# Four batches of a group through both attention layers in one sequence, the projections' row carried through DRAM

## Chip, cores and metric

The kernel runs on one core of a Trainium2 chip (trn2). The metric is device time in microseconds (us), the median of several runs; lower is better. Everything is computed in fp32. PE is the matrix engine, DVE the vector engine, ACT the scalar engine, POOL the engine that issues gathers and scatters here, SP the engine whose queue issues most plain DMAs.

## What is computed

The input is x (16 batches, 1024 nodes, 256 features) and one 1024 x 1024 adjacency matrix with about 17 entries a row. Four layers follow each other:

```python
# layer 0: a score for every edge, then sums over edges
S   = sigmoid(relu(x@W1[:d] (+) x@W1[d:] + b1) @ W2 + b2)      # per pair of nodes
x   = beta1*x + beta2*((S*adj)^T @ x @ Wa + ba) + beta3*(((adj^T @ x) * x) @ Wm + bm)
# layer 1
x   = x + relu((adj @ x) @ W^T + b)
# layers 2 and 3: attention over all pairs, adj as an additive bias
f   = x @ W1^T                       # features
f1  = f @ W2 + b2                    # one number a node: its projection
c   = softmax(leaky_relu(f1[i] + f1[j]) + adj)
x   = c @ f + bias2 + x
```

## The kernel before, in words

The 16 batches are handled in four groups of four (GB = 4). Three kinds of work share the core.

**The side work** (score_steps) computes the edge scores of layer 0. One step handles one edge slot of 128 nodes for the four batches of a group: POOL gathers 512 KB of neighbours' rows (L695), DVE adds and multiplies (L812, L814), ACT sums four times (L818), POOL scatters the scores into a dense matrix in DRAM (L700). There are 608 such steps, and 8 more that look for the slots. A step's gather is issued four steps ahead.

**The free part** (score_free) is dense matrix work of layer 0 that needs no scores, for all batches, on PE.

**The group part** runs for g = 0..3 once the scores of group g are in DRAM. with_edges multiplies the dense scores (DMA gd, turned into gc by ACT at L1072) with hw of four batches; its sums take all eight PSUM banks. Then pair_layers runs for batches 0 and 1 and again for 2 and 3: layer_one (projected, then neighbours, which reads adjT_in by DMA) and layers 2 and 3. For one batch and layer these consist of front (8 node tiles of features, 16 products of 257 columns; column 256 is the projection), scales and two calls of sums (v = 0, 1; 8 x 4 products each, on tiles m that DVE makes at L1044 from rho, tau and exp(adj)).

scales (L1003 to L1026) needs the projections of all nodes as a row on every partition (rho). It gets this by nine PE transposes of broadcast columns (eight at L1010 of feats, one at L1015 of their maxima), ACT evacuates two banks into rho (L1019), and exponentials and eight scalings of feats follow. finish at the end of sums divides by the softmax's sum: in layer 2 (second) the values are turned back by PE a little later (L1227), in layer 3 (third) z gets its bias, eight transposes of z (L1251) are issued after the last product, and the result goes out by a DMA on ACT's queue.

**Order.** The main work and the side work are Python generators. Side.along lets the main generator emit work, adds its own estimate of that work's us times a rate to what is owed, and emits so many side steps in between: 0.26 a us in the free part, 0.255 in all of the group part. Work that should not be emitted at once goes on a list, later, and catch_up emits all of it: at tile 1 of a front, or after tile 0 of a sums. A scheduler then puts the instructions into the engines' queues, roughly in that order but earlier where a tile is free and operands are there; each queue is served in order. paced ties a side step's DVE add, gc's copy and the loads of gd to a product on PE a few products back. For the next group, ahead loads hw and z of all four batches in the middle of the second pair; z's tiles are those of the current group (four tiles in all), so each load waits for its predecessor's last reader. gd has four tiles and is loaded by with_edges itself (only the first group's first four are loaded early). hw, y and feats share five tiles, rho has two, m four, adjT_in three.

The last group runs without side work, with another way for part of layer 1 (far_ahead, by_lists); its attention layers are the same pair_layers.

Of the kernel before, what the change touches and what calls it, by code (L numbers as in the profile page):

```python
# [13 lines left out]
ALU = mybir.AluOpType  # L14
# [5 lines left out]
RATE = (0.26, 0.255)  # L20
# [45 lines left out]
def gnn_stack_kernel(  # L66
# [120 lines left out]
    class Attention:  # L187


        def __init__(self, W1, W2, b2, bias2, name):  # L190
            self.W1 = W1
            self.w2 = column(W2, f"{name}_w2")
            self.b2 = everywhere(b2, 1, f"{name}_b2")
            self.bias2 = column(bias2, f"{name}_bias2c")
            self.wT = const.tile([P, DH, D + 1], F32, name=f"{name}_wT")
            self.rows = const.tile([P, DH, P], F32, name=f"{name}_rows")

        def prepare(self, nat):
# [8 lines left out]
            nc.vector.tensor_copy(self.wT[:, :, D], ps[:, :DH])  # L207
            for dh in range(DH):
                nc.vector.tensor_copy(self.rows[:, dh, :], self.wT[:, dh, D : D + 1].to_broadcast([P, P]))
# [26 lines left out]
    def prepare(t):  # L236
        transpose_weight(l1wT, t[:, 0])
        for i, gat in enumerate((gat2, gat3)):
            gat.prepare(t[:, 1 + i])
# [22 lines left out]
    part_d = dram.tile([XT * P + P, 2 * D], F32, name="part_d")  # L262

# [411 lines left out]
    with tc.If(listed > 0) as arm:  # L675
        with ExitStack() as stack:
# [192 lines left out]
            class Side:  # L869
# [5 lines left out]
                def along(self, main, rate=1):  # L875
                    for us in main:
                        self.owed += us * rate
# [35 lines left out]
            z_loads = []  # L913

            with ExitStack() as first:
# [48 lines left out]
                side.along(with_zeros(score_free()), RATE[0])  # L964
# [12 lines left out]
            def front(x, weights):  # L977

                wT = weights.wT
                f = ttile("feats").rearrange("p (t d) -> p t d", t=NT)  # L980
                for jt in range(NT):
# [7 lines left out]
                    if jt == 1:  # L989
                        catch_up()  # L990
                    yield 0.86
                made = {}
                later.append(lambda: scales(f, weights, made))
                return made

            def scales(f, weights, made):
# [4 lines left out]
                ta = small.tile([P, NT], F32, tag="tau", name="tau")  # L1001
# [16 lines left out]
                for v in range(NV):  # L1018
                    nc.scalar.activation(r[:, v * HN : (v + 1) * HN], banks[v], AF.Relu, bias=sh[:, 3:4])  # L1019
                nc.vector.tensor_scalar(sh[:, 1:2], sh[:, 0:1], -0.01, None, ALU.mult)  # L1020
# [8 lines left out]
            later = []  # L1029

            def catch_up():
                while later:
                    later.pop(0)()

            def sums(made, v, finish):

                if "f" not in made:
                    catch_up()
# [3 lines left out]
                for jt in range(NT):  # L1042
# [9 lines left out]
                    if jt == 0:  # L1052
                        catch_up()
# [10 lines left out]
            def with_edges(g, hw, z):  # L1064

                for v in range(N // QN):
# [33 lines left out]
            def projected(z, keep=None):  # L1100

                y = [node_major("y") for _ in range(2)]
# [24 lines left out]
            def neighbours(y, z, cols):  # L1127
                n = cols.stop - cols.start
                acc = [[bank() for _ in range(DH)] for _ in range(2)]
                for jt in range(NT):  # L1130
                    a = three.tile([P, HN], F32, tag="a", name="adjT_in")[:, :n]
                    nc.sync.dma_start(a, adjT_d[jt][:, cols])
                    for i in range(2):
                        for eh in range(DH):
# [3 lines left out]
                            )  # L1138
                    yield 3.4 * n / HN
# [66 lines left out]
            def pair_layers(b, z, ahead, first):  # L1206


                yield from first


                def second(i):
                    def finish(v, acc, share):
                        cols = slice(v * HN, (v + 1) * HN)
                        vals = []
                        for c in range(HT):
                            if c % 2 == 0:
                                pair = four.tile([P, 2, D], F32, tag="st", name="val")
                            val = pair[:, c % 2, :]
                            nc.scalar.activation(val, acc[c][:, :D], AF.Identity, scale=share[:, c : c + 1])  # L1220
                            vals.append(val)

                        def turn_back():
                            ps = [bank() for _ in range(DH)]
                            for c in range(HT):
                                for dh in range(DH):
                                    nc.tensor.transpose(  # L1227
                                        ps[dh][:, c * P : (c + 1) * P], vals[c][:, dh * P : (dh + 1) * P], ident
                                    )
                            for dh in range(DH):  # L1230
                                nc.vector.scalar_tensor_tensor(
                                    z[i][:, dh, cols], ps[dh], gat2.bias2[:, dh : dh + 1], z[i][:, dh, cols],
                                    ALU.add, ALU.add,
                                )
                        later.append(turn_back)
                    return finish


                def third(i):
                    def finish(v, acc, share):  # L1240
                        if v == 0:
                            for dh in range(DH):
                                nc.scalar.activation(
                                    z[i][:, dh, :], z[i][:, dh, :], AF.Identity, bias=gat3.bias2[:, dh : dh + 1]
                                )
                        for c in range(0, HT, 2):
                            ps = bank()
                            it = v * HT + c
                            for k in range(2):
                                for dh in range(DH):  # L1250
# [203 lines left out]
```

## Time and profile before

| what | us |
|---|---|
| median of 3 runs | 3181.08 (3177.64 to 3188.89) |
| the profiled execution | 3181.81 |
| its span, first to last instruction | 3180.1 |
| PE busy in it | 3117.1 |
| DVE busy | 2354.2 |
| ACT busy | 1946.7 |
| POOL busy | 1823.1 |
| granted PE clock | 0.994 of full |

The stages of the trace, from the span's start, in us: until 165 the start and the first group's inputs; 165 to 955 the free part with side work; then for each of groups 0, 1, 2 the edges (955 to 1139, 1526 to 1639, 2090 to 2203) and the two pairs (to 1526, 2090 and 2653); group 3's edges from 2653 to 2766, the rest of it to the end. Of a pair, about 68 us are layer 1 and about 150 the attention layers.

In lines of the profile, "out<-in" are the program's names, "x" the count, then busy us, mean ns of one, and the idle time of the engine just before these instructions with what ended it. A product in fp32 is recorded as two matmul rows; a transpose as one. Rows overlap: a row's duration is longer than the distance to the next row's start.

### The profile page before, as it was taken

How to read it: one execution, taken by the hardware profiler on the slowest of the kernel's cores; microseconds unless marked ns; L12 is line 12 of the kernel's file. 1: busy time of each engine (PE TensorE's matmuls, PEld its weight loads, DVE VectorE, ACT ScalarE, POOL GpSimd, SP SyncE). 2: the span in 40 equal slices, each digit the busy share in tenths (PEclk: the TensorE clock that was granted, in tenths of full speed). 3: DMA queues.
4: the chain of work that ended last, by engine and by line, in shares of the span. 5: the costliest groups of instructions: out<-in, count | busy, mean ns of one | idle time of the engine just before them, and what ended most of it. 6: DMA issues, size and time to landing. Idle time of an engine off the chain costs nothing.

```text
span 3180.1 us, 39242 instructions
## 1 busy us (share of the span) xinstructions
PE 3117.1 (98%) x12122; PEld 2198.4 (69%) x12122; DVE 2354.2 (74%) x3174; ACT 1946.7 (61%) x6512; POOL 1823.1 (57%) x1483
## 2 busy tenths in 40 slices
PE   8899999999999999999999999999999999999999
PEld 5444554545547768678876866888587688858888
DVE  7797777768775689889777978977798892147844
ACT  3245565656667877567886757788666774513342
POOL 1146778777665666767566665656676652067600
PEclk9999999999999999999999999999999999999999
DMA  9899798788889764766876576587657644476600
GB/s 314 292 324 327 253 304 278 257 256 251 259 284 332 226 185 136 225 189 198 294 240 177 155 205 188 181 294 238 193 142 216 187 133 159 133 253 170 165 7 28
DMA packets 281994, 687.48 MB, mean 216 GB/s; under 512 B 45280, under 2 KB 137440, under 8 KB 274608
## 3 DMA queue, kind: packets, MB, share of 16 engines
q0 software_dynamic: 128224, 387.80, 41.9%
q1 hardware_dynamic: 126112, 245.98, 22.4%
q10 hardware_dynamic: 27440, 51.13, 4.3%
q8 instruction: 97, 1.59, 0.2%
q14 instruction: 121, 0.99, 0.1%
HBM read 553.45 MB, written 131.32 MB: 215 GB/s over the span
## 4 chain that ended last, share of the span: by engine, by line
PE 78%; DVE 8%; DMA 6%; ACT 4%; issue 2%; POOL 1%; SPq 0%; ACTq 0%; DVEq 0%; POOLq 0%
PE bank L126 75%; DMA z<-v_d,slot_v 2%; DVE z L812 2%; ACT z L818 2%; DVE z L814 2%; ACT gc L1072 1%; DVE slot_a L440 1%; DMA gd<-dense_d 1%; PE bank L1227 1%; DVE left L442 1%; DVE m L1044 1%; PE bank L1010 1%; POOL z L695 1%; PE bank L1251 1%; POOL dense_d L700 1%
## 5 line engine op out<-in xcount | busy, mean ns | idle before, releaser
L818 ACT ACTIVATE z<-z 128x256 f32<-128x256 f32 x2432 | 979.9, 407 | 630.0 <-DVE z L814 611.1
L812 DVE TENSOR_TENSOR z<-z,u 128x1024 f32<-128x1024 f32 x608 | 738.6, 1220 | 416.6 <-PE bank L126 305.6
L126 PE MATMUL bank<-feats,m 128*128 128x257 f32 x4096 | 917.1, 381 | 5.2 <-DVE m L1044 4.5
L695 POOL DMA_INDIRECT z<-v_d,slot_v x512 | 644.3, 1258 | 447.0 <-ACT z L818 255.7
L126 PEld LDWEIGHTS bank<-feats,m 128*128 128x128 f32 x4096 | 767.7, 190 | 122.1 <-DVE m L1044 8.0
L700 POOL DMA_INDIRECT dense_d<-gt,slot_at x512 | 645.8, 1261 | 187.2 <-issue 135.8
L814 DVE SCALAR_TENSOR_TENSOR z<-z,w2r 128x1024 f32<-128x1024 f32 x608 | 737.7, 1219 | 9.0
L126 PE MATMUL bank<-gc,hw 128*128 128x256 f32 x2048 | 457.7, 385 | 23.2 <-ACT gc L1072 20.1
L818 ACT ACTIVATION_READ_ACCUMULATOR z<-z 128x1 f32 x2432 | 463.3, 191 | 0.0
L126 PEld LDWEIGHTS bank<-gc,hw 128*128 128x128 f32 x2048 | 389.7, 192 | 90.8 <-ACT gc L1072 30.6
L126 PE MATMUL bank<-adj_sb,h 128*128 128x512 f32 x1024 | 442.4, 592 | 2.8 <-ACT st L322 2.8
L1044 DVE SCALAR_TENSOR_TENSOR m<-rho,tau,adj_sb 128x512 f32<-128x512 f32 x512 | 375.1, 743 | 68.2 <-PE bank L126 65.0
L126 PE MATMUL bank<-adjT_in,y 128*128 128x512 f32 (+1 forms) x960 | 400.5, 578 | 1.5 <-DMA adjT_in<-adjT_d 1.5
L126 PEld LDWEIGHTS bank<-adj_sb,h 128*128 128x128 f32 x1024 | 194.3, 190 | 242.6 <-issue 237.5
L126 PE MATMUL bank<-w,hT 128*128 128x512 f32 (+1 forms) x1024 | 338.0, 491 | 0.0
L126 PEld LDWEIGHTS bank<-adjT_in,y 128*128 128x128 f32 x960 | 182.0, 190 | 215.7 <-issue 201.2
L1072 ACT ACTIVATE gc<-gd 128x1024 f32<-128x1024 f32 x128 | 264.9, 2072 | 94.0 <-PE bank L126 65.8
L126 PEld LDWEIGHTS bank<-w,hT 128*128 128x128 f32 x1024 | 196.6, 193 | 143.1 <-issue 120.8
L126 PE MATMUL bank<-g_wT,z 128*128 128x257 f32 x1024 | 231.1, 380 | 0.2 <-DVE z L1125 0.2
L695 POOL DMA_INDIRECT z<-v_d,x_node x96 | 120.8, 1258 | 176.8 <-ACT z L818 130.9
L126 PEld LDWEIGHTS bank<-g_wT,z 128*128 128x128 f32 x1024 | 191.6, 190 | 30.0 <-issue 2.9
L322 ACT ACTIVATE st<-bank 128x512 f32<-128x512 f32 x128 | 75.8, 592 | 101.2 <-PE bank L126 54.2
(161 smaller groups left out, 2400.7 us busy)
## 6 DMA issues: line engine op xcount, KB each, us to landing
gd<-dense_d SPq DMA_DIRECT2D x128, 512.0 KB, 4.8
dense_d<-zero ACTq DMA_DIRECT2D x64, 512.0 KB, 5.3
adjT_in<-adjT_d SPq DMA_DIRECT2D x112, 256.0 KB, 3.7
h<-in_x_dram SPq DMA_DIRECT2D x19, 1024.0 KB, 12.7
u_d<-st SPq DMA_DIRECT2D x64, 256.0 KB, 5.9
v_d<-st SPq DMA_DIRECT2D x64, 256.0 KB, 6.4
hw_d<-st SPq DMA_DIRECT2D x64, 256.0 KB, 7.0
u<-u_d POOLq DMA_DIRECT2D x32, 512.0 KB, 8.4
```

The costliest lines, as they stand in the source:

```text
L126: recent.append(nc.tensor.matmul(*args, **kw))
L322: nc.scalar.activation(st[:, c, :2, :], ps.rearrange("p (s k) -> p s k", s=2), AF.Copy)
L440: nc.vector.max(out=slot_a[:, t, s], in_=src)
L442: nc.vector.match_replace(out=left, in_to_replace=slot_a[:, t, s], in_values=src, imm_value=-1.0)
L695: return nc.gpsimd.indirect_dma_start(out=dst, out_offset=None, in_=src[:], in_offset=bass.IndirectOffsetOnAxis(ap=at, axis=0), **how,)
L700: return nc.gpsimd.indirect_dma_start(out=dst[:], out_offset=bass.IndirectOffsetOnAxis(ap=at, axis=0), in_=src, in_offset=None,)
L812: paced(nc.vector.tensor_tensor(z, z, u, ALU.add))
L814: nc.vector.scalar_tensor_tensor(zk, zk, 0.0, w2r[:, None, :].to_broadcast([P, GB, D]), ALU.max, ALU.mult)
L818: nc.scalar.activation(zk[:, c, :], zk[:, c, :], AF.Copy, accum_out=s[:, k, c : c + 1])
L1010: nc.tensor.transpose(ps[:, c * P : (c + 1) * P], f[:, jt, D : D + 1].to_broadcast([P, P]), ident)
L1044: nc.vector.scalar_tensor_tensor(m, r[:, cols], ta[:, jt : jt + 1], ea[:, jt, cols], ALU.max, ALU.mult)
L1072: paced(nc.scalar.activation(gc, gd.rearrange("p n i -> p i n"), AF.Copy), 16)
```

## The change

Five edits, all in the group part.

1. For groups 0 to 2, group_layers takes the place of two calls of pair_layers. It runs layer 1 of batches 0 and 1, the front of batch 0, layer 1 of batches 2 and 3, then eight times (layer 2 of four batches, layer 3 of four batches) the next front and the two sums of the current one.
2. The nine transposes of scales stay for a group's first front and for the last group. For the seven other fronts of groups 0 to 2 (21 in all) to_row makes one transpose of a 128 x 9 column, copies nine rows on ACT, writes them to DRAM (SP), reads them back as rho on all partitions and reads the maxima (SP, two DMAs). from_row, with the rest of scales, is emitted five ticks later. A tick comes at tiles 1 and 5 of a front, after tiles 0, 2, 4, 6 of a sums and after each tile of neighbours; entries of later now carry a count of ticks.
3. third's bias is added after tile 2 of v = 0, and its eight transposes are issued within the sums, after tiles 6 and 7, instead of behind them. This holds for the last group too.
4. hw and z of the next group are loaded within the last two batches of layer 3, and if the next group's scores are done by then, its first four gd too.
5. The rate of side steps depends on the stage: 0.225 in the edges, 0.288 in layer 1, 0.255 in fronts and sums, 0.26 in the free part.

The broadcast weights that only the fallback path reads are no longer kept in SBUF.

```diff
-RATE = (0.26, 0.255)
+PACE = dict(free=0.26, edges=0.225, one=0.288, fronts=0.255, sums=0.255)
...
-            self.rows = const.tile([P, DH, P], F32, name=f"{name}_rows")
+        def prepare(self, nat, pool=None):
...
+            if pool is None:
+                return
+            self.rows = pool.tile([P, DH, P], F32, name=f"{self.name}_rows")
...
+    row_d = dram.tile([2, B, (NT + 1) * P], F32, name="row_d")
...
-                def along(self, main, rate=1):
+                def along(self, main, pace=PACE):
                     for us in main:
-                        self.owed += us * rate
+                        self.owed += us * pace[doing[0]]
...
-            def front(x, weights):
-
+            later = []
+
+            def tick():
+                for what in later:
+                    what[0] -= 1
+                while later and later[0][0] <= 0:
+                    later.pop(0)[1]()
+
+            def catch_up():
+                while later:
+                    later.pop(0)[1]()
+
+            def front(x, weights, row=None):
+
+                doing[0] = "fronts"
...
                     nc.scalar.activation(f[:, jt, :], ps[:, : D + 1], AF.Copy)
-                    if jt == 1:
-                        catch_up()
+                    if jt % 4 == 1:
+                        tick()
                     yield 0.86
                 made = {}
-                later.append(lambda: scales(f, weights, made))
+                if row is None:
+                    later.append([1, lambda: scales(f, weights, made)])
+                else:
+                    later.append([1, lambda: to_row(f, weights, made, row)])
                 return made
+
+            def to_row(f, weights, made, row):
+
+                r = two.tile([P, N], F32, tag="rho", name="rho")
+                tops = two.tile([P, P], F32, tag="tops", name="tops")
+                column = small.tile([P, NT + 1], F32, tag="column", name="column")
+                nc.vector.tensor_copy(column[:, :NT], f[:, :, D])
+                nc.vector.tensor_reduce(column[:, NT:], f[:, :, D], AX.X, ALU.max)
+                ps = bank()
+                nc.tensor.transpose(ps[: NT + 1, :P], column, ident)
+                nc.scalar.activation(r[: NT + 1, :P], ps[: NT + 1, :P], AF.Copy)
+                nc.sync.dma_start(row.rearrange("(t p) -> t p", p=P), r[: NT + 1, :P])
+                nc.sync.dma_start(r, bcast_rows(row[:N], N))
+                nc.sync.dma_start(tops, bcast_rows(row[N:], P))
+                later.append([5, lambda: from_row(f, weights, made, r, tops)])
+
+            def from_row(f, weights, made, r, tops):
+                sh = small.tile([P, 4], F32, tag="shift", name="shift")
+                nc.vector.tensor_reduce(sh[:, 0:1], tops, AX.X, ALU.max)
+                nc.vector.scalar_tensor_tensor(sh[:, 3:4], weights.b2, 2.0, sh[:, 0:1], ALU.mult, ALU.add)
+                nc.scalar.activation(r, r, AF.Relu, bias=sh[:, 3:4])
+                scaled(f, made, r, sh)
 
             def scales(f, weights, made):
...
+                scaled(f, made, r, sh)
+
+            def scaled(f, made, r, sh):
...
-            later = []
-
-            def catch_up():
-                while later:
-                    later.pop(0)()
-
-            def sums(made, v, finish):
-
-                if "f" not in made:
-                    catch_up()
+            def sums(made, v, finish, early=None):
+
+                doing[0] = "sums"
+                while "f" not in made:
+                    tick()
                 f, r, ta = made["f"], made["r"], made["ta"]
...
-                    if jt == 0:
-                        catch_up()
+                    if jt % 2 == 0:
+                        tick()
+                    if early:
+                        early(v, jt)
...
+                    tick()
...
+            def third(z, i, b):
+                turned_back = []
+
+                def early(v, jt):
+                    if v == 0 and jt == 2:
+                        for dh in range(DH):
+                            nc.scalar.activation(
+                                z[i][:, dh, :], z[i][:, dh, :], AF.Identity, bias=gat3.bias2[:, dh : dh + 1]
+                            )
+                    if jt < NT - 2:
+                        return
+                    ps = bank()
+                    for k in range(2):
+                        it = v * HT + (jt - NT + 2) * 2 + k
+                        for dh in range(DH):
+                            nc.tensor.transpose(
+                                ps[:, k * D + dh * P : k * D + (dh + 1) * P],
+                                z[i][:, dh, it * P : (it + 1) * P], ident,
+                            )
+                    turned_back.append(ps)
+
+                def finish(v, acc, share):
...
+                return finish, early
...
-            def ahead(g):
-                if g < NGR:
-                    loaded.append(([load_hw(g * GB + i) for i in range(GB)], load_z(g)))
-                    for load, i in z_loads:
-                        load(i)
-                    z_loads.clear()
+            def group_layers(g, z):
+
+
+                made = {}
+
+                def fronts(layer, i, row=True):
+                    row = row_d[layer, g * GB + i] if row else None
+                    made[layer, i] = yield from front(z[i], (gat2, gat3)[layer], row)
+
+                order = [(layer, i) for layer in range(2) for i in range(GB)]
+                yield from layer_one(z[:2])
+                yield from fronts(0, 0, row=False)
+                yield from layer_one(z[2:])
+                for n, (layer, i) in enumerate(order):
+                    if n + 1 < len(order):
+                        yield from fronts(*order[n + 1])
+                    if n == 2 * GB - 2:
+                        hw, nz = [load_hw((g + 1) * GB + k) for k in range(GB - 1)], load_z(g + 1)
+                        for _ in range(2):
+                            load, k = z_loads.pop(0)
+                            load(k)
+                    ends = third(z, i, g * GB) if layer else (second(z, i),)
+                    yield from sums(made[layer, i], 0, *ends)
+                    if n == 2 * GB - 1:
+                        hw.append(load_hw((g + 1) * GB + GB - 1))
+                        load, k = z_loads.pop(0)
+                        load(k)
+                        soon(g + 1)
+                    yield from sums(made[layer, i], 1, *ends)
+                loaded.append((hw, nz))
+                assert not later
+
+            def soon(g):
+
+                if g in finished:
+                    first_gd.extend(load_gd(g, 0, ut) for ut in range(4))
...
-                side.along(with_edges(g, hw, z), RATE[1])
-                one = pair_layers(g * GB, z[:2], lambda: None, layer_one(z[:2]))
+                side.along(with_edges(g, hw, z))
                 if g < NGR - 1:
-                    side.along(one, RATE[1])
-                    side.along(pair_layers(g * GB + 2, z[2:], lambda: ahead(g + 1), layer_one(z[2:])), RATE[1])
+                    side.along(group_layers(g, z))
                 else:
-                    for _ in far_ahead(z[2:], one):
+                    for _ in far_ahead(z[2:], pair_layers(g * GB, z[:2], layer_one(z[:2]))):
                         pass
-                    for _ in pair_layers(g * GB + 2, z[2:], lambda: None, from_lists(z[2:], msg)):
+                    for _ in pair_layers(g * GB + 2, z[2:], from_lists(z[2:], msg)):
                         pass
```

## The prediction

> **What bounds the kernel now.** I read the page's first part, the groups, PE's timeline, its waits, the table of windows by stage, and the DMA issues, in this order.
>
> ```profile
> PE 3117.1 (98%) x12122; PEld 2198.4 (69%) x12122; DVE 2354.2 (74%) x3174; ACT 1946.7 (61%) x6512; POOL 1823.1 (57%) x1483
> ...
> L126 PE MATMUL bank<-feats,m 128*128 128x257 f32 x4096 | 917.1, 381 | 5.2 <-DVE m L1044 4.5
> ```
> ```profile
> L1010 PE MATMUL bank<-ident,feats 128*128 128x128 f32 x256 | 35.5, 274 | 0.0
> ```
> PE is the bound, but a row's 381 ns is not its price. The timeline shows the distances:
>
> ```profile
> 1160.97 1.03 PE L1010 MATMUL bank<-ident,feats 128*128 128x128 f32 x8
> 1161.84 0.27 PE L1015 MATMUL bank<-ident,top 128*128 128x128 f32 x1
> 1161.95 5.38 PE L126 MATMUL bank<-g_wT,z 128*128 128x257 f32 x24
> ...
> 1496.13 14.04 PE L126 MATMUL bank<-feats,m 128*128 128x257 f32 x64
> 1510.01 1.04 PE L1251 MATMUL bank<-ident,z 128*128 128x128 f32 x8
> ```
> 64 rows of 257 columns take 1510.01 - 1496.13 = 13.88 us, 0.217 each; eight transposes take 1161.84 - 1160.97 = 0.87 us, 0.109 each. In the same way 256 columns take 0.216 and 512 take 0.429. All rows at these distances: 5120 of 257 (1108), 3136 of 256 (676), 2688 of 512 (1153), 1155 transposes (126) and 22 narrow ones (2) are 3065 us. The first matmul starts at 4.8 us, the last one's start is 6.8 us before the end; the distances beyond the spacing are the other 103.6 us. That is all that better order can win. By stage they are: start 28.2, free part 6.4, edges of groups 0 to 3 17.0, 5.9, 8.5 and 7.6, the pairs of groups 0 to 2 25.6, the rest of the last group 4.4.
>
> Where the edges lose it is in PE's waits, and in the timeline of the start of group 3:
>
> ```profile
> PE bank L126 <- ACT gc L1072: 20.1, 13, 4.8
> ```
> ```profile
> 2652.27 1.27 SPq L894 DMA_DIRECT2D gd<-dense_d  x3
> 2652.32 1.04 PE L1251 MATMUL bank<-ident,z 128*128 128x128 f32 x8
> ...
> 2656.06 3.93 ACT L1072 ACTIVATE gc<-gd 128x1024 f32<-128x1024 f32 x2 [17.59 <-DMA gd<-dense_d]
> 2658.12 2.08 PE L126 MATMUL bank<-gc,hw 128*128 128x256 f32 x4 [4.76 <-ACT gc L1072]
> ```
> gd's loads are issued when the sums end, then ACT copies, then PE starts: 4.76 us of nothing. The stages differ in what else is full (PE, PEld, DVE, ACT, POOL busy):
>
> ```profile
> 955.00:1069.00 114.00, 103.95 (x456) 86.02 (x455) 62.32 (x73) 95.41 (x198) 54.89 (x45) 0.98 0.92 321
> ...
> 1376.00:1526.00 150.00, 149.49 (x727) 127.89 (x726) 142.51 (x211) 114.07 (x411) 106.74 (x75) 1.00 0.63 192
> 1526.00:1639.00 113.00, 109.26 (x502) 93.47 (x501) 77.96 (x93) 107.76 (x254) 71.78 (x61) 1.00 0.89 292
> 1639.00:1707.00 68.00, 68.00 (x200) 37.72 (x199) 48.76 (x53) 39.98 (x164) 39.74 (x35) 1.00 0.67 192
> ```
> In the edges ACT is 95% busy (107.76 of 113), in the attention stretch DVE is (142.51 of 150), in layer 1 neither (DVE 48.76 of 68).
>
> **What the skill says.** (1) Perfetto Trace Analysis, Identifying the Most-Contended Engine: matmul busy time is no good measure, because matmuls are pipelined. The trace agrees: 381 ns long, 217 apart. (2) TensorE: Matmul & The Clock Gate, Part 4: a transpose takes some 275 ns in a kernel. The trace has 274 as duration, but 109 in a row; I use 109. (3) DMA: Bandwidth & Descriptors, Anatomy of one DMA: some 2.0 us are fixed in each DMA, most of it the receipt of the write. The nearest row agrees: y_d<-y lands after 2.2.
>
> **The change, part by part.** Against the profiled execution's 3181.8 us.
>
> Transposes. 21 fronts lose nine and gain one: 21 x 8 x 0.109 = 18.3 us of PE, which is on the path wherever PE is full. Of the row's other work, DVE gets a copy and three small operations for as many small ones (0.16 to 0.29 us each): nothing. ACT's two reads of a bank (2 x 0.68) become a 9-row copy and one of 1024 columns (1.05, as L1022): nothing, ACT has 36 us of 150 free. **-18.3.**
>
> The edges' start. Group by group, gd's four tiles are loaded a sums (14 us) ahead; a load lands after 4.8 us in the median (the DMA issues' last column, us to landing), so gc can be made before the last product. For this the scores must be done: counting steps along the estimates, groups 1, 2 and 3 finish at steps 323, 475 and 615, and 346, 485 and 616 are emitted at the check. The transposes of third leave the end, too, and SP's queue no longer holds gd behind loads of z that wait for them. The rest of the edges' loss is ACT: at 0.225 instead of 0.255, 108.8 x 0.03 = 3.3 steps of about 1.6 us on ACT (four sums, 0.4 apart) go, 5 of 113 us. Of 22.0 us in groups 1 to 3 I leave 2.5 each: **-14.5.** In group 0, 89.6 x 0.03 = 2.7 steps go, but gd's DMAs are late too (DMA 92% busy), and they stay: of 17.0 I take off **-4.5.** If ACT isn't relieved, this and half of the former are gone.
>
> The steps that leave the edges go to layer 1: 0.288 instead of 0.255 a us. Per 68 us that is 2.2 steps, 5 us of DVE, which has 19 free, and 1.1 MB of gathers beside adjT_in, on DMAs 67 to 77% busy. In group 3's layer 1 PE loses 2.0 us to adjT_in. For six such stretches between 0 and 6: **+1.5.** Running layer 1 of the second pair earlier moves its adjT_in loads ahead in SP's queue, to where nothing else waits there.
>
> Loads of hw and z move to the last two batches, 1 MB each in SP's queue, ahead of the last front's row. Their tiles come free one batch after the other, so they don't come at once: between 0 and the 8 us by which a z lands, for each of three groups; counted with the row.
>
> The row's round trip, the new wait. DVE's maximum of tops and ACT's Relu stand in their queues until the DMAs land; behind them wait side steps and the m tiles that PE needs within four tiles (4 x 1.73 = 6.9 us). from_row comes five ticks after to_row: 5 x 3.47 = 17.3 us. The trip: write 2.2 (y_d) to 7.0 (hw_d), read of 512 KB 4.8 (gd's median) to 12.1 (its longest), some 1 us for transpose, copy and issues: 8 to 20 us. Mostly covered; the scheduler may place from_row earlier, and some trips will be late. Per trip 0 to 2.7 us, 21 times: 0 to 57; I take 0.2, **+4.**
>
> DVE in the long stretch. Its work per batch and layer stays, and PE needs less: 150 - 4 x 0.87 = 146.5 us for 142.5 of DVE, 97%. In two such stretches in a row no layer 1 lets DVE catch up. Between 0 and 15 (the 6.5 us of idle DVE that pacing needs stay: 149 - 146.5 = 2.5, six times): **+3.**
>
> third's early transposes do not change PE's sum. But they filled PE while ACT freed the banks for the next sums; ACT starts on a bank before the last product ends (three products of 0.43 follow it). Between 0 and 0.87 x 20 = 17: **+1.** The bias (1.15 us on ACT, twice) moves to tile 2 of the same sums, ahead of side steps there: nothing.
>
> Sum: -18.3 - 14.5 - 4.5 + 1.5 + 4 + 3 + 1 = -27.8, so 3154.0; the runs' median stands 0.7 lower than the profiled execution: **3153.**
>
> **Rivals.**
>
> A. The row's trip is late and the order reverses (slower). DVE is 95% busy there, so what it stands still, PE loses. If the trip takes 20.0 of the 17.3 us each time, 21 x 2.7 = 57 in place of my 4: 3153 + 53 = 3206. It decides from (27.8 + 4) / 21 = 1.5 us lateness a trip. For it: hw and z in the same queue, gathers on the same DMAs, DVE lags by a step or two when to_row comes. Against it: gathers four steps ahead (some 16 us) land in 5.6 and DVE waits for none of them in the pairs.
>
> B. DVE becomes the bound of the long stretch: 15 instead of 3, and rows that were covered show (3 more): 3168. For it: 97%. Against it: before, at 95%, PE lost 4.5 us to m in all.
>
> C. The edges don't gain, because ACT or the DMAs hold gc there whatever is loaded early: 3153 + 14.5 + 4.5 = 3172. For it: most waits for gc are not the first one (13 of them). Against it: 4.76 of group 3's 7.6 us are the first.
>
> D. All costs are nil and the attention stretch loses less as well (9.5 off, and 5 of its 25.6): 3139.
>
> **How the numbers follow.** Forecast 0.50 (3146 to 3162), A 0.14, B 0.14, C 0.12, D 0.10. 0.3% of 3181 is 9.5 us, about what a measurement can tell from no change. Faster by more is below 3171.5: the forecast, D, most of B, half of C and none of A, 0.75. Within: the rest of B and C and A's short trips, 0.13. Slower: 0.12. The range reaches from D to just short of A: 3138 to 3180, with about 0.17 left out.
>
> **What would show it.** 64 + 24 = 88 transposes at L1010's place and 11 at L1015's instead of 256 and 32, and 21 narrow ones: right for the first step. PE's wait for gc at the edges' starts under 1 us each: right for the second. DVE's or ACT's idle before tops or rho, ended by a DMA: rival A if over 1.5 us a trip. PE's wait for m over 15 us in all: B. Edges of groups 1 to 3 still losing over 15 us: C. The prediction is wrong if PE's distances beyond the spacing grow in the attention stretch by more than they shrink in the edges.

## The result, and the profile after

The changed kernel takes 3160.09 us in the median of six runs (3154.20 to 3162.65), beside 3179.36 for the kernel before in six runs. The ratio is 0.9935, 95% interval 0.9918 to 0.9953: faster by 0.65%, some 20 us, where 3153 or 28 us was forecast. The profiled execution took 3160.66 us, its span 3159.0, so 21.1 us less span than before.

From the page of the changed kernel, and from its groups of instructions (busy us, mean ns of one, and the engine's idle time before them with what ended it):

```profile
PE 3089.6 (98%) x11954; PEld 2178.2 (69%) x11954; DVE 2355.8 (75%) x3191; ACT 1954.7 (62%) x6512; POOL 1853.1 (59%) x1483
...
L128 PE MATMUL bank<-feats,m 128*128 128x257 f32 x4096 | 915.5, 381 | 12.8 <-DVE m L1089 7.1
```
```profile
L1056 PE MATMUL bank<-ident,feats 128*128 128x128 f32 x88 | 11.4, 273 | 0.0
...
L1038 DVE TENSOR_REDUCE shift<-tops 128x1 f32<-128x128 f32 x21 | 5.9, 279 | 15.3 <-DMA tops<-row_d 15.3
L1029 PE MATMUL bank<-ident,column 128*9 128x128 f32 x21 | 5.7, 271 | 1.3 <-DVE column L1027 1.2
...
L1061 PE MATMUL bank<-ident,top 128*128 128x128 f32 x11 | 3.1, 282 | 0.1
```
The first step of the forecast is there to the letter: 88, 11 and 21 transposes where 256 and 32 stood. But in front of the products of the attention layers PE now stands 12.8 us where it stood 5.2, and there is a new idle time, 15.3 us of DVE before tops.

PE's waits (us in total, times, longest):

```profile
PE bank L128 <- ACT st L1312: 8.4, 13, 1.5
PE bank L128 <- ACT gc L1120: 8.2, 11, 2.0
...
PE bank L1273 <- ACT val L1266: 7.4, 6, 2.2
PE bank L128 <- DVE m L1089: 7.1, 8, 2.3
```
The wait for gc has fallen from 20.1 to 8.2 us; the waits for st (from 2.1), val (from 1.1) and m (from 4.5) have grown. (st is layer 3's result on its way out, val layer 2's values before they are turned back; ACT makes both out of the banks of a finished sums.) The timeline of the start of group 3's edges in the changed kernel:

```profile
2619.59 1.43 POOL L708 DMA_INDIRECT dense_d<-gt,slot_at  x1 [0.30 <-issue]
...
2622.28 2.21 SPq L902 DMA_DIRECT2D gd<-dense_d  x4
...
2629.41 2.06 ACT L1120 ACTIVATE gc<-gd 128x1024 f32<-128x1024 f32 x1 [6.32 <-PE bank L128]
...
2636.59 5.78 PE L128 MATMUL bank<-gc,hw 128*128 128x256 f32 x26
```
gc is made 7 us before PE needs it, and PE goes on without a gap. The table by stage (edges of group 0, 294 us of fronts and sums of group 0, edges of group 1, layer 1 of group 1; PE, PEld, DVE, ACT, POOL busy, then the granted PE clock, the DMA engines' busy share and their GB/s):

```profile
953.00:1067.00 114.00, 108.35 (x481) 91.17 (x480) 57.58 (x67) 95.38 (x186) 46.16 (x40) 0.99 0.91 317
1223.00:1517.00 294.00, 286.56 (x1373) 245.84 (x1372) 281.29 (x427) 219.59 (x803) 213.64 (x151) 1.00 0.66 199
1517.00:1630.00 113.00, 112.31 (x514) 96.10 (x513) 73.50 (x90) 105.42 (x241) 68.69 (x58) 1.00 0.85 276
1630.00:1698.00 68.00, 66.84 (x189) 35.50 (x188) 52.44 (x52) 41.26 (x169) 44.12 (x35) 1.00 0.70 202
```
DVE is 96% busy over the long stretch (281.29 of 294), as thought.

The prediction's account of PE (rows at their usual start-to-start distance, and by stage what the distances have beyond it) can be drawn up for both traces, and again for a second pair: both kernels were run once more as controls, on one chip (further down). Each stage goes from its first to its last product; group 0's edges end at 1083 us in the kernel before, and the 1139 named ahead of the prediction takes in most of a layer 1.

| us of span | forecast | first pair | control pair |
|---|---|---|---|
| transposes at 0.109 | -18.3 | -18.3 | -18.3 |
| edges of groups 0 to 3, with their starts | -19.0 | 39.0 to 19.2 | 39.4 to 19.4 |
| layer 1 and attention of groups 0 to 2 | +9.5 | 25.6 to 42.7 | 25.5 to 39.4 |
| last group | 0 | 4.4 to 7.3 | 4.2 to 4.7 |
| start and free part (no edit touches them) | 0 | 34.6 to 32.2 | 37.4 to 30.4 |

The row of the transposes is a count times a distance (168 at 0.109); the others are measured. The two gains have the size of the forecast. The costs in layer 1 and attention were put at 9.5 and came to 17.1 and 13.9.

One part of these losses has no name in the prediction: rows that PE runs at half the granted clock. At the start of group 3 in the kernel before, PE's first four rows take 2.08 us (the last line of the prediction's timeline), where three distances of 0.216 and one row of 0.38 make 1.03; most rows of this stretch are 0.427 us apart. The same stretch in the table of windows, clock third from the end:

```profile
2655.70:2662.50 6.80, 4.17 (x9) 2.92 (x10) 1.37 (x2) 5.38 (x6) 0.00 (x0) 0.50 0.93 353
```
So the 7.6 us of that start are 4.76 and 0.20 us of standing still, and the rest mostly slow rows. By an estimate from the traces (half of the time that PE ran at a granted clock of 0.50), slow rows cost the edges 7.2 and 6.7 us in the two traces of the kernel before, and 1.7 and 0.0 in those of the changed one; PE's standing still there fell from 23.2 to 9.5 and from 23.9 to 11.6. About a third of the gain of the edges is thus clock. In these four traces each slow stretch of the edges, of layer 1 and of attention is 3.4 or 6.8 us long and begins during a stop of PE or within about 1 us of its end; not every stop has one (in the changed kernel, those of 2.2 us at 1298 and 2.1 us at 1930 have none), and no run asked what decides.

The experiments ask where the costs of layer 1 and attention came from, and whether the gain of the edges has the cause that was given for it.

### The profile page after: what moved, and what is told of

Its sections match the earlier page's. It is cut to its first block, busy times and chain, and to the rows that moved or that the text cites. A ratio compares the mean times of both kernels' runs of the same rounds, so it can differ in the third digit from the quotient of the medians.

```text
span 3159.0 us, 38968 instructions
## 1 busy us (share of the span) xinstructions
PE 3089.6 (98%) x11954; PEld 2178.2 (69%) x11954; DVE 2355.8 (75%) x3191; ACT 1954.7 (62%) x6512; POOL 1853.1 (59%) x1483
## 5 line engine op out<-in xcount | busy, mean ns | idle before, releaser
L128 PE MATMUL bank<-feats,m 128*128 128x257 f32 x4096 | 915.5, 381 | 12.8 <-DVE m L1089 7.1
L703 POOL DMA_INDIRECT z<-v_d,slot_v x512 | 652.1, 1274 | 434.8 <-ACT z L826 249.7
L128 PEld LDWEIGHTS bank<-feats,m 128*128 128x128 f32 x4096 | 767.9, 190 | 128.7 <-DVE m L1089 13.4
L708 POOL DMA_INDIRECT dense_d<-gt,slot_at x512 | 665.8, 1300 | 192.7 <-issue 128.9
```

Source lines behind the costliest of these rows:

```text
L128: recent.append(nc.tensor.matmul(*args, **kw))
L703: return nc.gpsimd.indirect_dma_start(out=dst, out_offset=None, in_=src[:], in_offset=bass.IndirectOffsetOnAxis(ap=at, axis=0), **how,)
L708: return nc.gpsimd.indirect_dma_start(out=dst[:], out_offset=bass.IndirectOffsetOnAxis(ap=at, axis=0), in_=src, in_offset=None,)
```

## Experiments

Each set of four ran on one chip, each set on a different one, with runs of the kernel before in between. The kernel before took 3179 us with the first pair and 3198, 3207 and 3180 us in sets one, two and three, so across sets ratios to it are compared; us of one trace against those of another set carry the difference of the chips. "Pairs" is short for PE's distances beyond the spacing in layer 1 and the attention layers of groups 0 to 2, "edges" for those in the edges with their starts.

### Set one: one edit undone at a time

No row through DRAM:

```diff
-                    row = row_d[layer, g * GB + i] if row else None
+                    row = None
```


> The changed kernel with the nine transposes in every front, so no row goes through DRAM. Theory (the row's trip saves PE's 18.3 us and gives back a part, because DVE stands 15.3 us before tops and a third or so of it reaches PE): 11 to 14 us slower than the changed kernel, 0.9970 to 0.9980 of the kernel before; PE's distances beyond the spacing fall by 4 to 7 us in the attention stretch. Rival (DVE is so full there that all it stands is lost by PE): within 4 us of the changed kernel, 0.994 to 0.995. Second rival (the trip is free): 17 to 19 us slower, about 0.999.

Measured: 0.9950 (0.9932 to 0.9967), 3183.3 beside 3197.6 us; pairs 27.2 us, where the changed kernel has 42.7 and 39.4. PE hardly waits for m in this kernel:

```profile
L128 PE MATMUL bank<-feats,m 128*128 128x257 f32 x4096 | 916.5, 381 | 1.3 <-DVE m L1089 0.8 <-ACT st L1312 0.2
```
Without the trip the long stretch costs PE hardly more than the two shorter ones did before (27.2 against 25.5 us, on another chip), with the same side work. Against the two traces of the changed kernel, the trip gives back 12 to 15.5 of its 18.3 us; the three other kernels of this set, which have the trip, lose 36 to 45 us in pairs, 9 to 18 more than this one. By the ratios, whose intervals overlap, leaving it out makes the kernel 2.5 to 5 us slower. All this is nearer to the first rival than to the theory, and the long stretch at 96% DVE is hardly a cost of its own. (In this trace the edges lose 27.9 us, 13.4 of them in group 2; the two others of this set with the new rates lose 22.6 and 27.1, so the ratio is not the trip's net gain to the microsecond.)

Layer 3's transposes behind the last product:

```diff
                 def early(v, jt):
...
-                    if jt < NT - 2:
-                        return
-                    ps = bank()
...
-                    turned_back.append(ps)
...
-                        ps = turned_back.pop(0)
+                        ps = bank()
                         it = v * HT + c
+                        for k in range(2):
+                            for dh in range(DH):
+                                nc.tensor.transpose(
...
```


> The changed kernel with layer 3's eight transposes behind the last product again. Theory (the early transposes cost bank waits, since PE has nothing left to do while ACT frees the accumulators): PE's wait for ACT's st (8.4 us) falls to about 2 and the kernel is 3 to 7 us faster than the changed one, about 0.992 of the kernel before. Rival (the early transposes help, because the edges' first products no longer stand behind them): 2 to 6 us slower, 0.9945 to 0.9955, lost at the starts of the edges of groups 1 to 3.

Measured: 0.9928 (0.9904 to 0.9953). PE's wait for st is 4.3 us instead of 8.4, as the theory has it, but its wait for m is 10.0. The ratio doesn't separate the two readings; what is sure is that the early transposes gain nothing that can be measured. (In set three the wait for st falls to 2.9 us with the early transposes left in, so most of it is not theirs.)

One rate in all of the group part:

```diff
-PACE = dict(free=0.26, edges=0.225, one=0.288, fronts=0.255, sums=0.255)
+PACE = dict(free=0.26, edges=0.255, one=0.255, fronts=0.255, sums=0.255)
```


> The changed kernel with 0.255 a us in the edges and in layer 1. Theory (in the edges ACT is the bound, and the lower rate gave about half of their 20 us): edges lose 7 to 11 us more than in the changed kernel, layer 1 up to 3 less, 5 to 8 us slower in all, 0.9955 to 0.996. Rival (the edges gained by the early loads alone): within 2 us of the changed kernel.

Measured: 0.9954 (0.9937 to 0.9971). The edges lose 41.3 us, as many as before (39.0), though z's loads are out of the way and gd's are issued 17 us ahead of the first product in groups 1 and 2. In group 3, 7.4 us are lost, where 7.6 were before. PE waits 20.8 us for gc, as before the change:

```profile
PE bank L128 <- ACT gc L1120: 20.8, 14, 4.4
```
No early gd:

```diff
-                        soon(g + 1)
```


> The changed kernel with the first four gd of groups 1 to 3 loaded by the edges themselves again. Theory (the early loads took away the first wait of the edges): 2.5 to 5 us more at the start of each of the three edges, 8 to 12 us slower, 0.9965 to 0.9975. Rival (the loads were already early enough once z's loads no longer stand ahead of them in SP's queue, or the scheduler moves them ahead itself): within 2 us of the changed kernel.

Measured: 0.9930 (0.9914 to 0.9946), edges 22.6 us. The rival holds: the edges of group 3 lose 0.2 us with the early loads and 0.2 without them, and those of groups 1 and 2 together 2 to 3 more than in the two traces of the changed kernel. The timeline of this kernel shows the scheduler's own early load:

```profile
2632.64 7.26 SPq L902 DMA_DIRECT2D gd<-dense_d  x3
2636.11 2.06 ACT L1120 ACTIVATE gc<-gd 128x1024 f32<-128x1024 f32 x1 [6.35 <-PE bank L128]
...
2643.29 2.97 PE L128 MATMUL bank<-gc,hw 128*128 128x256 f32 x13
```
What sets group 3's start is the side work. gd can't be read before the group's last scatter; the last scatter and the first gd stand at 2650.0 and 2652.3 us in the kernel before, at 2619.6 and 2622.3 in the changed one, at 2648.1 and 2650.4 with one rate, and at 2626.3 and 2632.6 here. Counted from the first product of the edges, the last scatter is 8 us ahead before and with one rate, 17 us in the two kernels with the new rates. Lower in the edges and higher in layer 1, these rates come to more steps in sum (an estimate from the prediction's figures: 3.3 fewer and twice 2.2 more a group), so that the side work is done before the last sums.

### Set two: what in the trip costs, and the rates alone

tops read ahead of rho:

```diff
-                nc.sync.dma_start(r, bcast_rows(row[:N], N))
                 nc.sync.dma_start(tops, bcast_rows(row[N:], P))
+                nc.sync.dma_start(r, bcast_rows(row[:N], N))
```


> The changed kernel with the read of tops (64 KB) ahead of the read of rho (512 KB) in SP's queue. Theory (PE pays for the row because DVE stands in its queue until tops land behind rho): DVE's wait for tops falls from 15.3 us to under 4, PE's excess in the attention stretch by 5 to 12 us, 4 to 9 us faster than the changed kernel, 0.991 to 0.992 of the kernel before. Rival (the trip costs PE something else: ACT's wait for rho, or more work for ACT): the wait only moves to ACT, within 2 us of the changed kernel, about 0.9935.

Measured: 0.9928 (0.9909 to 0.9946). DVE's wait for tops fell to 9.0 us in 5 trips, not under 4, and pairs stayed at 44.2 us: distances of 2.0, 2.1, 2.5 and 1.7 us too much still stand in front of tiles 1 and 2 of the second half of sums, one put down to m and three to st. The traces show one reason: the scheduler, too, placed the maximum earlier, 10.8 us after the write in the median, 12.0 in the changed kernel. The theory of the cost isn't refuted by this, but the remedy was wrong.

All at once, at six ticks:

```diff
-                while later and later[0][0] <= 0:
-                    later.pop(0)[1]()
+                for what in [w for w in later if w[0] <= 0]:
+                    later.remove(what)
+                    what[1]()
...
-                later.append([5, lambda: from_row(f, weights, made, r, tops)])
+                later.append([6, lambda: from_row(f, weights, made, r, tops)])
```
(with the edits of the late transposes and of tops first)

> The changed kernel with tops read first, the second half at six ticks instead of five (and a tick no longer holding turn_back behind it), and layer 3's transposes behind the last product. Theory: the row's cost and the bank waits both go, 8 to 14 us faster than the changed kernel, 0.989 to 0.991 of the kernel before. Rival (what PE loses there is DVE at 97% whatever waits): within 3 us of the changed kernel.

Measured: 0.9956 (0.9938 to 0.9973), a miss on both sides: 3191.5 us, 10 above the former kernel on the same chip, and by the ratio no faster than the changed kernel. DVE still waits 10.1 us for tops, and PE's wait for val is 21.5 us in place of 7.4:

```profile
PE bank L1274 <- ACT val L1267: 21.5, 17, 3.1
```
A reading that fits, but that no run isolates: at six ticks ACT's block behind the maximum (Relu, exponentials, eight scalings, about 6 us) comes just ahead of val at the end of sums.

The new rates in the kernel before, nothing else (each generator sets doing, and along takes PACE[doing[0]] in place of RATE):

```diff
-                        self.owed += us * rate
+                        self.owed += us * pace[doing[0]]
```


> The kernel before with the five new rates alone. Theory (the rates made the edges' gain, the early loads none: less ACT work in the edges, and the last scatters of a group done earlier): edges of the four groups lose 19 to 24 us instead of 39, the group 3 edges start at once, 12 to 18 us faster than before, 0.9945 to 0.996. Rival (it takes the new order of loads as well, because z's loads stand ahead of gd in SP's queue): 5 to 8 us faster, 0.9975 to 0.9985.

Measured: 0.9955 (0.9940 to 0.9970), 13.6 us, the time that the theory has. By the ratios, the rates alone make two thirds of the whole change's gain, and the change without them makes about as much (0.9954 above), so the two don't simply add up. Group 3's edges start at once (0.2 us lost, 7.6 before). In groups 1 and 2, though, the edges lose 26.5 us in this trace, where they lost 14.4 before; ACT waits 14.4 us for gd there. The edges of all four groups lose some 39.5 us, so the theory's 19 to 24 there is a miss. The trace is that of the slowest of the nine runs (3200.9 us), and the kernel before has no trace in this set, where its time is 27 us above that of the first pair, so the 13.6 us can't be placed stage by stage. What stands is that neither the rates alone (39.5) nor all other edits without them (41.3) lower the edges' loss from 39.0, and both together do (19.2). The rates are needed; what else is, probably the later place of the loads of hw and z, wasn't tried by itself.

The second half after two ticks:

```diff
-                later.append([5, lambda: from_row(f, weights, made, r, tops)])
+                later.append([2, lambda: from_row(f, weights, made, r, tops)])
```


> The changed kernel with the second half of the row two ticks after the first instead of five (7 us instead of 17). Theory (a late trip stops DVE and so PE): DVE waits 2 to 6 us in each of the 21 trips, 40 to 120 us in all, and at least half of it reaches PE: 20 to 60 us slower than the changed kernel, 1.000 to 1.012 of the kernel before. Rival (the scheduler places the second half where the data is expected whatever the ticks): within 4 us of the changed kernel.

Measured: 1.0081 (1.0057 to 1.0105), slower than the kernel before. The tile view of tops:

```profile
L1038 DVE TENSOR_REDUCE shift<-tops x21: 282/286/290, 1246.6 to 2664.0; 128x1 f32<-128x128 f32 x21
its engine sat idle before it (us, times) until:
  DMA tops<-row_d: 45.5, 18
```
The maximum stands 8.7 us behind the write in the median, DVE waits in 18 of 21 trips, and pairs rise to 101.6 us, 18.6 of them slow rows by the same estimate. In these 18 trips tops land 6.4 to 12.7 us after the write is issued, 8.8 in the median. Rival A of the prediction names a real mechanism; at five ticks it has only a part of its size.

### Set three: controls and the remedy

Both kernels themselves:

> The kernel before itself, as a control: its trace on the chip on which the changed kernel and the next two run, since the distances beyond the spacing differ between chips. Every theory: 1.000 within 0.2%; the last group may lose some 8 us more here than in the first trace, as all experiments on other chips did.

> The changed kernel itself, as a control on the same chip. Theory: 0.9925 to 0.9945 of the kernel before; against the control before, edges lose 15 to 20 us less and the pairs of groups 0 to 2 12 to 18 us more, 10 to 16 of it in waits for m at tiles 0 to 5 of the second half of sums, where DVE stands before tops.

Measured: 1.0008 (0.9998 to 1.0018) for the kernel before, 0.9942 (0.9925 to 0.9958) for the changed one; the account is in the table above. The changed kernel's pairs lose 13.9 us more than those of the kernel before, as forecast, but by another way in part: PE's waits for m are 4.6 us, where 10 to 16 were expected, those for st 8.2 and for val 7.1, and slow rows make 5.1 us (1.7 before). The last group doesn't lose the 8 us here that it lost in the other two sets (11.3 to 13.5 us and 11.7 to 13.5 us in the traces of sets one and two, 4.2 to 9.2 here).

The maximum held back by a wait on PE:

```diff
-                nc.vector.tensor_reduce(sh[:, 0:1], tops, AX.X, ALU.max)
+                paced(nc.vector.tensor_reduce(sh[:, 0:1], tops, AX.X, ALU.max))
```


> The changed kernel with DVE's maximum of tops tied to the product on PE six products back, so that the scheduler can't put it ahead of its place at the fifth tick. Theory (the scheduler places the maximum 9 to 14 us after the write in place of the 17 of the ticks, and DVE stands there until tops land): DVE's wait for tops falls from 15 to under 3 us, PE's waits for m in the second half of sums from some 12 to under 4, 6 to 11 us faster than the changed kernel, 0.9900 to 0.9915 of the kernel before. Rival (a later maximum only moves ACT's block of Relu, exponentials and eight scalings onto the end of sums, where val and st wait for ACT, as with six ticks): PE's wait for val rises by what m's falls, within 3 us of the changed kernel.

Measured: 0.9903 (0.9885 to 0.9920), 3149.59 us beside 3158.95 for the changed kernel on the same chip. Pairs are 26.8 us, where the changed kernel has 39.4 and the kernel before 25.5. One trip shows how. DVE's timeline in the changed kernel:

```profile
2428.10 0.74 DVE L1089 SCALAR_TENSOR_TENSOR m<-rho,tau,adj_sb 128x512 f32<-128x512 f32 x1
2428.76 1.22 DVE L822 SCALAR_TENSOR_TENSOR z<-z,w2r 128x1024 f32<-128x1024 f32 x1
2429.90 1.53 DVE L1089 SCALAR_TENSOR_TENSOR m<-rho,tau,adj_sb 128x512 f32<-128x512 f32 x2
2436.79 0.29 DVE L1038 TENSOR_REDUCE shift<-tops 128x1 f32<-128x128 f32 x1 [5.36 <-DMA tops<-row_d]
...
2438.44 0.75 DVE L1089 SCALAR_TENSOR_TENSOR m<-rho,tau,adj_sb 128x512 f32<-128x512 f32 x1
```
and PE's, where the two gaps follow:

```profile
2429.83 7.75 PE L128 MATMUL bank<-feats,m 128*128 128x257 f32 x35
2439.24 2.00 PE L128 MATMUL bank<-feats,m 128*128 128x257 f32 x8 [1.66 <-DVE m L1089]
2443.57 3.01 PE L128 MATMUL bank<-feats,m 128*128 128x257 f32 x7 [2.33 <-DVE m L1089]
```
The same trip on DVE with the maximum held:

```profile
2429.31 1.21 DVE L820 TENSOR_TENSOR z<-z,u 128x1024 f32<-128x1024 f32 x1
...
2431.76 2.07 DVE L1089 SCALAR_TENSOR_TENSOR m<-rho,tau,adj_sb 128x512 f32<-128x512 f32 x3
2433.75 0.28 DVE L1038 TENSOR_REDUCE shift<-tops 128x1 f32<-128x128 f32 x1
```
In the first, 5.36 us of DVE become 1.66 + 2.33 = 3.99 us of PE, because the m tiles were queued behind. And that is not all: behind the second gap the granted clock is halved,

```profile
2444.00:2447.40 3.40, 3.40 (x11) 2.65 (x10) 3.29 (x7) 3.40 (x14) 1.11 (x1) 0.50 0.54 154
```
and seven rows take 3.01 us where eight took 2.00 before it. From 2437 to 2448 us PE's distances are 6.2 us too long in sum. In the same trip with the maximum held, the side step and three m tiles come first, and the data is there. Over all 21 trips the maximum stands 15.1 us behind the write in the median, 13.2 at the least, and DVE waits for tops in none:

```profile
L1038 DVE TENSOR_REDUCE shift<-tops x21: 223/276/286, 1248.7 to 2582.7; 128x1 f32<-128x128 f32 x21
its engine sat idle before it (us, times) until:
  PE bank L128: 0.3, 1
```
The rival, that ACT's block only moves onto val, fails: PE's wait for val is 5.5 us, 7.1 in the control. The wait for st falls from 8.2 to 2.9, that for m from 4.6 to 2.4, and slow rows in pairs from 5.1 us to none; 1.7 of these 5.1 follow a stop of 2.1 us that both traces have, so they are chance. (The two traces differ by only 4.0 us of span: free part, edges and last group, where this edit does nothing, lose 8.7 us more in the second, and the control's trace is that of its fastest run.)

The same with the late transposes:

> The former one with layer 3's transposes behind the last product as well. Theory (the early transposes neither help nor cost more than 2 us, as measured by themselves): within 2 us of the former. Rival (with the m waits gone, the waits for banks come to the fore, and the late transposes cover them): 3 to 6 us faster than the former.

Measured: 0.9893 (0.9875 to 0.9911), 3145.17 us, the fastest of all. It is 4.4 us below the former, as its rival has it, but the intervals overlap and pairs are 27.9 us in place of 26.8, so that the banks are the cause isn't shown; PE's wait for st is 3.2 us, not less than the 2.9 of the former.

## Why the prediction was right, and where it was off

Of the signs set down in advance, those of the rivals stayed away: DVE's idle time before tops is 0.7 us a trip (15.3 / 21; rival A from 1.5), PE's wait for m 7.1 us (B from 15), the edges of groups 1 to 3 lose some 8 us (C from 15), and pairs grew by 17.1 and 13.9 us where the edges shrank by 19.8 and 20.0, so the first pair is not far from the sign of being wrong. The sign of the second step, PE's wait at the edges' starts, came true (at most 0.6 us of standing still in the first 5 us of each), but not for the reason given.

**Transposes, -18.3.** Right, with the distance of 0.109 us and not the duration of 0.27 as price. The account has 107.6 us of transposes instead of 125.9.

**The edges, -14.5 and -4.5.** Right in sum (-19.8 and -20.0), and that is luck, since the cause was wrong for the larger part. The step "gd's four tiles are loaded a sums (14 us) ahead" was given the starts; without these loads group 3 starts just as early behind its last sums. Group 3's start, the 4.76 us that I read as a load issued too late, was a load that had to wait for the last scatter: the line of 2652.27 us told when it was issued, and POOL's timeline would have told why. "The rest of the edges' loss is ACT" left out the slow rows, 7 of the 39 us. I counted the rates as the smaller half, and without them none of the edges' gain is left; but the one trace with the rates alone doesn't show that gain either.

**Rates in layer 1, +1.5.** What PE loses in layer 1 of groups 0 to 2 went from 0.5 to 3.0 us, in the control from 0.4 to 1.5: right in size.

**The row's trip, +4.** The term that was mis-sized. With the maximum held back it is measured as 39.4 - 26.8 = 12.6 us of PE, some 11 without the slow rows called chance above; the kernel without the trip says 9 to 18. The step that failed is "Mostly covered", which rests on "from_row comes five ticks after to_row: 5 x 3.47 = 17.3 us". That is the place in the program; the scheduler brought DVE to the maximum 12.0 us behind the write in the median, 5.7 at the least. The trip itself was no longer than the 8 to 20 us it was put at: where DVE stood waiting, tops landed after 6.4 to 13.1 us. The sentence that it "may place from_row earlier" was there, and got 0.2 us a trip; it is 12.6 / 21 = 0.6, a part of it slow rows behind the stops, a term that the prediction doesn't have. Rival A's price would have been 2.7, and 1.5 would have eaten the gain; in the kernel with two ticks it is about 3.5 ((101.6 - 27.2) / 21, across two chips).

**DVE in the long stretch, +3, and rival B.** The load was right (96%), the cost is hardly there: with the maximum held, on the chip of the controls, pairs lose 26.8 us, 1.3 more than in the kernel before, and that holds the rates and the early transposes too. B falls.

**The early transposes, +1.** Their time is not settled, since the differences are less than the intervals. The wait for st, which rose to 8.4 us, is not theirs for the larger part: with the maximum held it is 2.9 us with them and 3.2 without.

In sum the forecast lay 7 us low (3153 against 3160). The trip's term was 8.6 too small; the other three of layer 1 and attention, 5.5 together, were some 4 too large by the controls, so two errors hid a part of each other.

## What to carry to other kernels

An operation whose data comes by DMA is, on an engine that is nearly full, as dear as the place where the scheduler puts it: look up in the trace how long behind the issue it really stands, and hold it there with a dependency on other work, not by emitting it later. Price a stop of PE with what follows it: in the trip shown, 3.99 us of standing still cost 6.2. Where a stage starts late, find what the load itself had to wait for before loading it earlier. Side work at different rates by stage, after the engine that is full in each, gave by itself two thirds of the gain of a change that had four other parts, as far as times tell; its trace doesn't show where.

## What the runs showed of the hardware that was not expected

The kernel before took 3179 to 3207 us in the four sets, a difference of 0.9% for the same code and more than the effect in question; sets one to three ran on three different chips, and whether chip or hour makes it wasn't asked. The ratios of the changed kernel in two of them (0.9935 and 0.9942) agree. A stop of PE of some 2 us is in part of the cases followed by 3.4 us at a granted clock of 0.50, with rows 0.427 apart instead of 0.217. The start and the free part, whose code no edit touches, lose between 30.3 and 37.4 us in the fourteen traces, 4.1 to 7.2 of it as slow rows; no run asked why.
